# Layer 1's attention: two of four rows of probabilities transposed by VectorE and DMA instead of TensorE, with a fixed order of TensorE's work

## The chip, the cores and the metric

The kernel runs on one core of one Trainium2 chip. The core has five engines with queues of their own, each working through its instructions in order: TensorE (matrix products; PE in the profile, PEld for its weight loads), VectorE (DVE), ScalarE (ACT), GpSimd (POOL) and SyncE (SP, which only issues DMAs here). Engines wait for one another through semaphores. Tiles live in SBUF; TensorE writes to PSUM, of which this kernel makes eight banks of 128 x 512 float32. The metric is the device time of one execution in microseconds; lower is better. All data are float32.

## The reference, cut to what matters

Four layers over x of 4 x 512 x 256; each normalises x and adds an attention part and a feed-forward part that both read the same normalised x. Layer 1 has latent attention with 16 heads and, beside it, a gated feed-forward net together with a lookup of eight "experts" per token. The change is in its attention:

```python
# L1_attn: b = 4 sequences, s = 512 tokens, 16 heads, latent width 64, rope width 64
q = rmsnorm(x @ wq_a) @ wq_b              # 16 heads of 128 + 64
ckv = x @ wkv_a                           # latent 64 and rope keys 64, shared by all heads
kv = rmsnorm(ckv[..., :64]) @ wkv_b       # keys and values of each head
scores = einsum('bqhd,bkhd->bhqk', qf, kf) * 192 ** -0.5     # qf, kf: nope | rotated rope
probs = softmax(where(causal, scores, -inf))
out = einsum('bhqk,bkhd->bqhd', probs, v) @ wo

# L1_ffn: product-key lookup (8 of 512 experts per token) plus a gated net
x = x + L1_attn(xn) + L1_ffn(xn)
```

## The kernel before

**Streams.** Layer 1 is written as Python generators that issue instructions and yield an estimated cost. `weave` always advances the stream that is least far through its own total: the attention (`latent_pieces`, 457), the expert lookup (`product_key_pieces`, 237), the gated net (`glu_units`, 126) and, near the end, the first routing of layer 2 (`room`). A scheduler then orders the instructions of each engine by this order and by when it expects operands; an order may be forced with `tc.keep_in_program_order`, or with `c.chain`, which ties each instruction to the last chained one. In the kernel before, layer 3 alone uses `c.chain`.

**Attention.** The weights of keys and values are folded into the queries and the output, so all heads attend over the same latent keys `kf` and values `cv` (64 wide). The loop over s runs through 64 heads of one sequence each (4 groups of heads x 4 sequences x 2 pairs x 2). Two heads make a pair: `queries` (L1072 to L1085) projects for both, ScalarE copies the result to `pes`, four DMAs swap its halves into `psw`, and `rotate` (L1091 to L1094) applies the rotary embedding. Per head, four rows of blocks i = 0..3 ("rows one to four") have scores of 128, 256, 384 and 512 keys (L985). `exp_scores` takes the masked minimum on VectorE (L988) and the exponent with its sum on ScalarE (L992); a reciprocal (L1108) and ScalarE (L1110) scale the row to probabilities `pr0`..`pr3`.

**Transposes.** The product with the values needs the probabilities with keys on partitions. `turned` does this on TensorE for all ten 128 x 128 blocks (L1117), one column of blocks per PSUM bank `tr`, and copies each bank to `PT` (L1121) on VectorE (columns 0 and 2: 512 and 256 wide) or ScalarE (384 and 128 wide). After the second head of a pair, eight wide products give z of both heads, one head in each half of the bank (L1253):

```python
z[h * KL : (h + 1) * KL, j * P :], lhsT=cv[:, b * TPB + j, :],
rhs=PTs[s - 2 + h][:, START[j] : START[j] + SEQ - j * P],
```

ScalarE scales z into `zT` (L1259), and after every second pair the output product (L1267) is added to x on VectorE (L183).

**Beside it.** The expert lookup first routes on VectorE, then for 16 tiles of tokens gathers eight expert rows each by indirect DMA on GpSimd's queue into tiles `e` (L1371, eight buffers), takes eight dot products on VectorE (L1381) and adds eight scaled rows to x on VectorE (L177); each addition frees an `e` buffer for the next tile's gather. The gated net's products are L159 and L237.

**Layer 3** already transposes the probabilities by VectorE and DMA: VectorE turns 32 x 32 blocks into `Y` (L1598), four SyncE DMAs write `Y` to DRAM (L1603), and a fifth reads it back as `PT` (L1607); its value products are 128 wide (L1642).

Of the kernel before, what the change touches and what calls it, by code (L numbers as in the profile page):

```python
# [16 lines left out]
P = 128  # L17
NB, SEQ, DM = 4, 512, 256
# [12 lines left out]
class Ctx:  # L31


    def __init__(self, tc, stack):
        self.tc, self.nc = tc, tc.nc
        self.stack = stack
        self.n = 0
        pool = lambda name, **kw: stack.enter_context(tc.tile_pool(name=name, **kw))
        self.keep = pool("keep", bufs=1)
        self.ln = pool("ln", bufs=1)  # L40
        self.psum = pool("psum", bufs=4, space=bass.MemoryType.PSUM)
        self.users, self.then, self.later, self.pinned = {}, None, [], False
        self.trickle, self.chained = [], None

    def tile(self, pool, shape, tag, dtype=F32, **kw):
        self.n += 1
# [11 lines left out]
    def chain(self, ins):  # L58


        last, self.chained = self.chained, ins.ins
        if last is not None:
            self.tc.add_manual_dep(
                ins.ins, last.name,
                mybir.DependencyInfo(mybir.DependencyClass.NoSync, mybir.DependencyReason.DATA),
                reason="chain",
            )
        return ins
# [942 lines left out]

def latent_pieces(c, a, keep, open_pool):

# [45 lines left out]
    def queries(p):  # L1063

        g, b, pair = p // 8, p // 2 % 4, p % 2
        if p % 8 == 0:
            carry(g)
        wpe0, wpe1, wl0, wl1, _ = weights[g]
        tokens = slice(b * SEQ, (b + 1) * SEQ)
        cols = slice(pair * P, (pair + 1) * P)  # L1070
        pe, pl = c.ps(), c.ps()
        nc.tensor.matmul(pl, lhsT=wl0[:, cols], rhs=qa0[:, tokens], start=True, stop=False)  # L1072
        upper = nc.tensor.matmul(pe, lhsT=wpe1[:, cols], rhs=qa1[:KL, tokens], start=True, stop=False)
        with tc.issue_after(upper.ins), tc.high_priority(offset=200):
            nc.tensor.matmul(pl, lhsT=wl1[KL:, cols], rhs=qa1[KL:, tokens], start=False, stop=True)
        with tc.high_priority(offset=100):
            nc.tensor.matmul(pe, lhsT=wpe0[:, cols], rhs=qa0[:, tokens], start=False, stop=True)

        pes, psw = (c.tile(pool, [P, SEQ], n, bufs=1) for n in ("pes", "psw"))
        nc.scalar.copy(pes, pe)  # L1080
        for to in range(0, P, 32):
            nc.sync.dma_start(psw[to : to + 32, :], pes[to ^ 32 : (to ^ 32) + 32, :])
        qf = c.tile(pool, [P, 2, SEQ], "qf")
        nc.scalar.mul(qf[:KL, 0, :], pl[:KL, :], -scale)
        nc.scalar.mul(qf[KL:, 1, :], pl[KL:, :], -scale)  # L1085
        qfs[p] = qf
        return pes, psw, qf

    def rotate(pes, psw, qf):
        pec = c.tile(pool, [P, SEQ], "pec", bufs=1)  # L1090
        nc.vector.tensor_mul(pec, pes, cosq)  # L1091
        tc.keep_in_program_order(nc.vector.tensor_mul(psw, psw, sinq))
        nc.vector.tensor_add(qf[:KL, 1, :], pec[:KL, :], psw[:KL, :])
        nc.vector.tensor_add(qf[KL:, 0, :], pec[KL:, :], psw[KL:, :])  # L1094

    def probabilities(s, i):
        p, h = s // 2, s % 2
        b = p // 2 % 4
        if i == 0:
            totals[s] = c.tile(pool, [P, TPB], "total")  # L1100
        rinv = totals[s]
        prs[s].append(exp_scores(
            c, pool, late, qfs[p][:, h, :], kf[:, h, b * SEQ : (b + 1) * SEQ], i, rinv[:, i : i + 1]
        ))
        if i >= TPB - 2:

            done = slice(0, i + 1) if i < TPB - 1 else slice(i, i + 1)
            nc.vector.reciprocal(rinv[:, done], rinv[:, done])  # L1108
            for j in range(TPB)[done]:
                nc.scalar.mul(prs[s][j], prs[s][j], rinv[:, j : j + 1])  # L1110

    def turned(s, j):

        pt = c.ps("tr")
        n = SEQ - j * P
        for i in range(j, TPB):
            nc.tensor.transpose(  # L1117
                pt[:, (i - j) * P : (i - j + 1) * P], prs[s][i][:, j * P : (j + 1) * P], c.ident
            )
        copy = nc.scalar.copy if j % 2 else nc.vector.tensor_copy  # L1120
        return lambda: copy(PTs[s][:, START[j] : START[j] + n], pt[:, :n])  # L1121

    START = (0, 512, 896, 1152)
    qfs, prs, totals, PTs, zTs = {}, {}, {}, {}, {}
    rope = c.tile(pool, [P, SEQ], "psw", bufs=1)
    nc.scalar.dma_start(rope, a["l_rope"])
# [2 lines left out]
    def latents(b):  # L1129

        if b < 2:
            rooms = [c.tile(pool, [P, 1280], "PT")[:, :1024]]
        elif b == 2:
            rooms = [c.tile(pool, [P, SEQ], "zT", bufs=3) for _ in range(2)]
        else:
            rooms = [c.tile(pool, [P, 2, SEQ], "qf").rearrange("p a b -> p (a b)")]
        return [v3(r, QL + KL)[:, t, :] for r in rooms for t in range(TPB // len(rooms))]
# [35 lines left out]
    for b in range(NB):  # L1173
        tokens = slice(b * SEQ, (b + 1) * SEQ)
        lats.append(latents(b))
        for t in range(TPB):
            tt = b * TPB + t
            pl = c.ps()[:, : QL + KL]
            project_tokens(c, pl, wa, slice(0, QL + KL), slice(tt * P, (tt + 1) * P))
            lat = lats[b][t]  # L1180
            nc.vector.tensor_copy(lat, pl)
            sq = c.tile(pool, [P, QL + KL], "pr1")
            nc.scalar.activation(
                sq[:, :QL], lat[:, :QL], AF.Square, accum_out=ms[:, 0, tt : tt + 1]
            )
            nc.scalar.activation(
                sq[:, QL:], lat[:, QL:], AF.Square, accum_out=ms[:, 1, tt : tt + 1]
            )
            yield 0.85
            if t == 1 and b > 0:  # L1190
                yield from rotary_keys()

        pk = c.ps()
        project(c, pk, wa, slice(256, 384), tokens)
        rot = c.tile(pool, [P, SEQ], "pr3")
        nc.vector.tensor_mul(rot, pk, rope)
        rots.append((rot, tokens))
        yield 1.2
# [16 lines left out]
        finish(b)  # L1215
        yield 1.9

    copy = None
    yield 1.9
    for s in range(65):  # L1220
        if s < 64:
            prs[s] = []
        for i in range(TPB):
            if s < 64:
                probabilities(s, i)
            if s > 0:
                if i == 0:
                    PTs[s - 1] = c.tile(pool, [P, 1280], "PT")
                ready, copy = copy, turned(s - 1, i)
                if ready:  # L1230
                    ready()
            if i == 0 and s % 2 == 1 and s < 63:
                rotate(*turning)
            yield 0.85
            if i == 1 and s % 2 == 0 and s < 62:
                turning = queries(s // 2 + 1)
                yield 2.6
        if copy:
            copy()
            copy = None  # L1240
        if s > 0:
            del prs[s - 1]
        if s % 2 == 1:
            continue
        if s == 0:
            continue

        p = s // 2 - 1
        g, b, pair = p // 8, p // 2 % 4, p % 2
        z = c.ps("acc")  # L1250
        for j in range(TPB):
            for h in range(2):
                tc.keep_in_program_order(nc.tensor.matmul(  # L1253
                    z[h * KL : (h + 1) * KL, j * P :], lhsT=cv[:, b * TPB + j, :],
                    rhs=PTs[s - 2 + h][:, START[j] : START[j] + SEQ - j * P],
                    start=(j == 0), stop=(j == TPB - 1),
                ))
        zTs[pair] = c.tile(pool, [P, SEQ], "zT", bufs=3)
        nc.scalar.mul(zTs[pair], z, kv_w)  # L1259
        yield 2.1  # L1260
        if pair == 1:
            wz = weights[g][4]
            for t in range(0, TPB, 2):
                po = v3(c.ps("acc"), DM)
                for j in range(2):
                    for k in range(2):
                        nc.tensor.matmul(  # L1267
                            po[:, j, :], lhsT=zTs[k][:, (t + j) * P : (t + j + 1) * P],
                            rhs=wz[:, k, :], start=(k == 0), stop=(k == 1),
                        )  # L1270
                add_pair(c, b * TPB + t, po)
                if g == 3 and t == TPB - 2:
                    c.part_done(b)
                yield 1.7


def product_key_pieces(c, a, keep, pool, dram, xn):
# [131 lines left out]
def layer1(c, a, xn, following):  # L1409


    with ExitStack() as stack, ExitStack() as right:
# [4 lines left out]
        glu = pool_of("g1", 1)  # L1417
        dram = pool_of("p_dram", 1, space=bass.MemoryType.DRAM)
        keep = pool_of("l_keep", 1)
        latent = latent_pieces(c, a, keep, lambda: pool_of("l_h", 2))  # L1420

        def glu_units():
            same = dict(tanh=True, bufs=5)
# [989 lines left out]
```

## Time and profile before

| | |
|---|---|
| median of 10 runs | 2938.59 us (2935.44 to 2944.33) |
| the profiled execution | 2938.87 us, of which the span of its instructions is 2937.1 us |
| layer 1's heads in it | first scores 854 us, last value product 1476 us |
| 862 to 1029 us | before the expert gathers' dot products; VectorE busy 131.5 of 167 us |
| 1029 to 1404 us | dot products and gathers; VectorE busy 306.8 of 375 us |
| 1404 to 1476 us | last heads; VectorE busy 46.8 of 72 us |

Times in the profile are those of one execution, in us, single instructions in ns. A group's line reads: line of the kernel, engine, operation, output tile <- input tiles, shapes, count | busy us, mean ns of one | idle time of the engine before them, with what ended it. A float32 product is two instructions (two passes); a transpose is one. The chain of waits follows the work that ended last back through what released it. "us to landing" of a DMA counts from its issue to the arrival of its data.

### The profile page before, as it was taken

What the parts mean: (1) busy time and instruction counts of PE and PEld (TensorE: products, weight loads), DVE (VectorE), ACT (ScalarE), POOL (GpSimd) and SP (SyncE); (2) the same over time, 40 slices, a digit from 0 to 9 for tenths busy, and PEclk for the clock granted to TensorE, in tenths of its full rate; (3) what the DMA queues carried; (4) which work ended last, traced back from release to release, by engine and by line L of the source; (5) the groups of instructions that cost most, each with busy time, mean ns of one, the idle gap of its engine ahead of it and who ended that gap; (6) DMA issues with size and microseconds to landing.
All of it is one profiled execution on the core that took longest, in us unless ns stands there. A gap on an engine that the chain in (4) does not pass through costs nothing.

```text
span 2937.1 us, 40559 instructions
## 1 busy us (share of the span) xinstructions
PE 2883.5 (98%) x13812; PEld 1954.8 (67%) x13812; DVE 2134.5 (73%) x5434; ACT 1391.2 (47%) x3336; POOL 858.3 (29%) x681
## 2 busy tenths in 40 slices
PE   8999999999999999999999999999999999999999
PEld 5666665666755655555677688888888756666666
DVE  6877778787778787878765877777777666666666
ACT  4444445354376666667633554544454333333332
POOL 0565655656410033333035200000000043333331
PEclk9999999999999999999999999999999999999999
DMA  3333332332320134444235434444444200000000
GB/s 134 100 100 122 100 110 94 105 122 83 115 68 15 56 102 131 106 106 111 77 91 162 150 113 126 138 133 128 147 122 148 94 1 22 22 22 22 22 1 29
DMA packets 138366, 268.03 MB, mean 91 GB/s; under 512 B 19664, under 2 KB 99040, under 8 KB 133808
## 3 DMA queue, kind: packets, MB, share of 16 engines
q1 hardware_dynamic: 123696, 217.65, 23.7%
q0 software_dynamic: 14176, 47.01, 6.3%
q8 instruction: 109, 1.79, 0.2%
q14 instruction: 97, 0.79, 0.1%
q10 hardware_dynamic: 288, 0.79, 0.1%
HBM read 202.21 MB, written 54.26 MB: 87 GB/s over the span
## 4 chain that ended last, share of the span: by engine, by line
PE 84%; DVE 7%; ACT 3%; DMA 2%; POOL 1%; issue 1%; SPq 0%; ACTq 0%; DVEq 0%; POOLq 0%
PE mm L329 17%; PE mm L159 14%; PE mm L985 7%; PE acc L329 7%; PE tr L329 6%; PE acc L1642 5%; PE acc L1001 4%; PE tr L823 3%; PE acc L1253 2%; PE mm L167 2%; PE acc L237 2%; PE tr L237 2%; PE acc L801 2%; PE tr L1117 2%; PE acc L1267 1%; PE mm L2036 1%
## 5 line engine op out<-in xcount | busy, mean ns | idle before, releaser
L992 ACT ACTIVATE pr<-pr,nm 128x128 f32<-128x128 f32 (+3 forms) x512 | 286.1, 559 | 295.2 <-DVE nm L988 292.4
L988 DVE CUSTOM_DVE_ANT_0 pr<-mm,late 128x128 f32<-128x128 f32 (+3 forms) x512 | 245.4, 482 | 114.1 <-PE mm L985 112.4
L159 PE MATMUL mm<-xnT,wu 128*128 128x512 f32 x624 | 288.4, 600 | 0.0
L340 ACT COPY part<-mm 128x512 f32<-128x512 f32 (+1 forms) x372 | 177.8, 479 | 213.2 <-PE mm L329 205.1
L329 PE MATMUL mm<-token_sums,unit_sums 128*128 128x512 f32 (+1 forms) x624 | 267.5, 511 | 2.2 <-ACT part L340 2.2
L1371 POOL DMA_INDIRECT e<-in_p_experts,ids x128 | 130.6, 1021 | 464.6 <-DVE x L177 323.5
L159 PE MATMUL mm<-xnT,w_in 128*128 128x512 f32 x512 | 229.2, 593 | 0.6 <-DVE cy L591 0.6
L491 DVE SCALAR_TENSOR_TENSOR x<-acc,cw,x 128x128 f32<-128x128 f32 x372 | 128.7, 346 | 108.1 <-PE acc L329 106.5
L591 DVE SCALAR_TENSOR_TENSOR cy<-mm,ws,cy 128x509 f32<-128x509 f32 (+2 forms) x216 | 160.1, 744 | 51.5 <-ACT cy L587 47.5
L159 PEld LDWEIGHTS mm<-xnT,wu 128*128 128x128 f32 x624 | 115.8, 193 | 118.4 <-issue 110.4
L985 PE MATMUL mm<-kf,qf 128*128 128x128 f32 (+3 forms) x512 | 174.3, 443 | 3.4 <-DVE qf L1094 3.1
L761 POOL TENSOR_TENSOR G<-G,CB 128x1024 f32<-128x1024 f32 x64 | 151.5, 2367 | 82.1 <-DVE G L724 76.0
L744 ACT ACTIVATE xD<-xc,ws 128x128 f32<-128x128 f32 x256 | 83.9, 390 | 191.8 <-POOL y L785 182.4
L985 PE MATMUL mm<-k,q 128*128 128x128 f32 (+3 forms) x512 | 170.4, 437 | 3.7 <-DVE q L1542 3.4
L329 PEld LDWEIGHTS acc<-down_sums,hidden_sums 128*128 128x128 f32 x744 | 112.1, 192 | 85.1 <-issue 83.4
L159 PEld LDWEIGHTS mm<-xnT,w_in 128*128 128x128 f32 x512 | 96.5, 190 | 104.4 <-issue 94.9
L1642 PEld LDWEIGHTS acc<-PT,V 128*128 128x128 f32 x1280 | 154.5, 194 | 8.2 <-issue 4.9
L1642 PE MATMUL acc<-PT,V 128*128 128x128 f32 x1280 | 154.9, 277 | 3.5 <-DMA PT<-turned 3.5
L273 POOL TENSOR_TENSOR down_sums<-wu 128x256 f32<-128x256 f32 x8 | 5.9, 741 | 520.6 <-DMA wu<-in_o_units 520.6
L724 DVE TENSOR_TENSOR_SCAN G<-G,eye 128x1024 f32<-128x1024 f32 x64 | 148.1, 2315 | 0.0
L474 DVE TENSOR_TENSOR whole<-mm,part 128x512 f32<-128x512 f32 x128 | 88.5, 692 | 68.5 <-PE mm L329 68.1
L1117 PEld LDWEIGHTS tr<-con,pr 128*128 128x128 f32 x640 | 79.5, 142 | 83.0 <-issue 19.7
(440 smaller groups left out, 6770.8 us busy)
## 6 DMA issues: line engine op xcount, KB each, us to landing
turned<-Y SPq DMA_DIRECT2D x252, 160.0 KB, 2.6
PT<-turned SPq DMA_DIRECT2D x63, 640.0 KB, 3.9
G<-own SPq DMA_DIRECT2D x64, 512.0 KB, 4.5
w_in<-in_m_units SPq DMA_DIRECT2D x16, 1024.0 KB
eb<-since SPq DMA_DIRECT2D x96, 128.0 KB, 3.4
wu<-in_o_units SPq DMA_DIRECT2D x6, 1536.0 KB, 6.5
wo<-in_m_units SPq DMA_DIRECT2D x16, 512.0 KB, 13.0
psw<-pes SPq DMA_DIRECT2D x128, 64.0 KB, 3.2
```

What stands on the lines that cost most here:

```text
L159: c.nc.tensor.matmul(out, lhsT=w[:, d, cols], rhs=c.xnT[:, d, tokens], start=(d == 0), stop=(d == 1))
L329: self.kept(self.c.nc.tensor.matmul(bank, lhsT=lhsT, rhs=rhs, start=first, stop=True, skip_group_check=not first))
L340: self.c.nc.scalar.copy(r, bank)
L591: nc.vector.scalar_tensor_tensor(y[:, j:], src[:, : SEQ - j], conv[:, k, 3 - j : 4 - j], y[:, j:], ALU.mult, ALU.add,)
L724: tc.keep_in_program_order(nc.vector.tensor_tensor_scan(flat, flat, eye.rearrange("p h t -> p (h t)"), 0.0, ALU.mult, ALU.add))
L761: nc.gpsimd.tensor_mul(G, G, seqs[b][2][:, t, :][:, None, :].to_broadcast([P, HG, P]))
L985: kept(nc.tensor.matmul(sc, lhsT=q[:, i * P : n], rhs=k[:, :n], start=True, stop=True))
L988: nc.vector.tensor_tensor_reduce(out=pr, in0=sc, in1=late[:, SEQ - n :], scale=scale, scalar=-NEG, op0=ALU.add, op1=ALU.min, accum_out=nm,)
L992: nc.scalar.activation(pr, pr, AF.Exp, bias=nm, scale=-1.0, accum_out=total)
L1117: nc.tensor.transpose(pt[:, (i - j) * P : (i - j + 1) * P], prs[s][i][:, j * P : (j + 1) * P], c.ident)
L1371: nc.gpsimd.indirect_dma_start(out=e, out_offset=None, in_=a["p_experts"], in_offset=bass.IndirectOffsetOnAxis(ap=ids[:, t, k : k + 1], ax ...
L1642: kept(nc.tensor.matmul(zs[:, i], lhsT=head["V"][:, j, h, :], rhs=head["PT"][:, :, i * (i + 1) // 2 + j, :], start=(j == 0), stop=(j == i),))
```

## The change

- Rows three and four of each head's probabilities (seven of ten blocks) are no longer transposed by TensorE. `turn_strips` has VectorE turn 32 x 32 blocks into `Y`, SyncE write `Y` to DRAM in four DMAs, and GpSimd issue the DMA that reads it back into `PT`. The last head (s = 63) keeps TensorE for these rows.
- Rows one and two (three blocks) stay on TensorE, in one bank, copied by ScalarE. VectorE no longer copies from `tr`.
- All TensorE instructions of the attention are chained in program order, with `c.chain` now keeping one chain per engine; the four writes are chained on SyncE too. `queries` takes its two banks from `tr` instead of `mm`.
- The product with the values is now 20 products of 128 columns per pair, placed between the third and fourth scores of the odd head after next, and the output products follow in two pieces in the next even head.
- `pr0`..`pr3` have one buffer each, `PT` three, `Y` one, `zT` two; `rotate` works in place; the reciprocal is taken over two rows at a time.

```diff
-        last, self.chained = self.chained, ins.ins
+        last = self.chained.get(ins.ins.engine)
+        self.chained[ins.ins.engine] = ins.ins
...
-        pe, pl = c.ps(), c.ps()
...
+        pe, pl = c.ps("tr"), c.ps("tr")
+        for out, lhsT, rhs, start, stop in (
+            (pl, wl0[:, cols], qa0[:, tokens], True, False),
+            (pe, wpe1[:, cols], qa1[:KL, tokens], True, False),
+            (pl, wl1[KL:, cols], qa1[KL:, tokens], False, True),
+            (pe, wpe0[:, cols], qa0[:, tokens], False, True),
+        ):
+            c.chain(nc.tensor.matmul(out, lhsT=lhsT, rhs=rhs, start=start, stop=stop))
...
-        if i >= TPB - 2:
-            done = slice(0, i + 1) if i < TPB - 1 else slice(i, i + 1)
+            kept=c.chain, bufs=1,
+        if i % 2:
+            done = slice(i - 1, i + 1)
...
+    def wide(tile, i):
+        lo = 0 if i == 2 else 3
+        return tile[:, :896].rearrange("p (a j s) -> p j a s", j=7, s=32)[:, lo : lo + i + 1]
+    def turn_strips(s, i):
+        if i == 2:
+            Ys[s] = c.tile(pool, [P, 896], "Y", bufs=1)
+        nc.vector.transpose(wide(Ys[s], i), strips(prs[s][i]))
+        if i == TPB - 1:
+            room = c.tile(dram, [4, 32, 4, 224], "strips")
+            PTs[s] = c.tile(pool, [P, 1280], "PT", bufs=3)
+            Y = Ys.pop(s)
+            for a in range(4):
+                c.chain(nc.sync.dma_start(
+                    room[:, :, a, :].rearrange("b r e -> r b e"),
+                    Y[a * 32 : (a + 1) * 32].rearrange("p (b e) -> p b e", b=4),
+                ))
+            nc.gpsimd.dma_start(PTs[s][:, :896], room.rearrange("b r a e -> (b r) (a e)"))
+    def turned(s, rows):
...
+                c.chain(nc.tensor.transpose(
+                    pt[:, n * P : (n + 1) * P], prs[s][i][:, j * P : (j + 1) * P], c.ident
+                ))
...
+            return lambda: nc.scalar.copy(PTs[s][:, 896:], pt[:, : 3 * P])
...
+    def values(p):
+        z = c.ps("acc")
+        for i in range(TPB):
+            for j in range(i + 1):
+                for h in range(2):
+                    c.chain(nc.tensor.matmul(
+                        z[h * KL : (h + 1) * KL, i * P : (i + 1) * P], lhsT=cv[:, b * TPB + j, :],
+                        rhs=block(2 * p + h, i, j), start=(j == 0), stop=(j == i),
+                    ))
...
+    for s in range(66):
...
+            if i == 0:
+                if s % 2 == 1 and s < 63:
+                    rotate(*turning)
+                yield from islice(pieces, 1)
+            if i == 1 and s % 2 == 0:
+                yield from islice(pieces, 1)
+                if s < 62:
+                    turning = queries(s // 2 + 1)
+                    yield 2.6
+            if i == 2 and s % 2 == 1 and s > 2:
+                pieces = values(s // 2 - 1)
+                yield 2.6
+            if i == TPB - 1 and s < 63:
+                turn_strips(s, 2)
+                turn_strips(s, 3)
+            if s < 64 and i == TPB - 1:
+                copy = turned(s, (0, 1))
+            if s == 64 and i < 2:
+                copy = turned(63, (i + 2,))
```

## The prediction

> **What bounds the kernel now.** The page first: it gives the span of the one profiled execution, to which the sum is made (with 1.8 us outside it, 2938.87 us, 0.3 us above the median of 2938.59, so the two are used as one).
>
> ```profile
> span 2937.1 us, 40559 instructions
> PE 2883.5 (98%) x13812; PEld 1954.8 (67%) x13812; DVE 2134.5 (73%) x5434; ACT 1391.2 (47%) x3336; POOL 858.3 (29%) x681
> ```
>
> The change touches only layer 1's attention, whose 64 heads run from about 854 to 1476 us, so next the windows: before, during and after the stretch in which GpSimd gathers experts (columns: busy us and instructions of PE, PEld, DVE, ACT, POOL, then clock, DMA share, GB/s).
>
> ```profile
> 862.00:1029.00 167.00, 162.91 (x759) 98.10 (x758) 131.49 (x490) 110.22 (x300) 0.00 (x0) 0.99 0.12 33
> 1029.00:1404.00 375.00, 365.76 (x1620) 208.77 (x1619) 306.78 (x1040) 251.46 (x673) 123.05 (x121) 1.00 0.43 109
> 1404.00:1476.00 72.00, 70.37 (x348) 45.40 (x346) 46.78 (x166) 47.08 (x120) 0.55 (x1) 0.93 0.23 77
> ```
>
> TensorE looks 98% busy, but its ends are modelled. The chain of waits shows its real rate: four transposes 0.44 us, so 0.11 each; a 512-column pass 0.43. Adding up the columns streamed between 855 and 1476 us at these rates gives 538 of 621 us. So TensorE is the largest load (87%), VectorE the second (82% in the gather stretch), and the rest is latency. The chain of waits of the gather stretch says which:
>
> ```profile
> by line: PE mm L985 11.3%; PE acc L1253 8.7%; PE mm L159 8.6%; PE tr L1117 7.4%; DMA psw<-pes 6.9%; PE acc L1267 5.9%; PE acc L237 5.6%; ACT pr L992 4.6%; ACT pr L1110 4.0%; issue 3.6%; PE mm L1073 3.1%; DVE pr L988 3.1%; PE mm L1072 2.8%;
> ```
>
> A DMA holds 6.9% and the softmax steps on ScalarE and VectorE some 12%. By the timeline the widest scores of heads 1, 17 and 55 end at 862.8, 1028.0 and 1386.5 us: a pair of heads takes 20.6 us ahead of the gathers and 18.9 in them.
>
> **The change, part by part.**
>
> *TensorE.* Of ten transposes per head the seven of rows three and four go, in 63 heads: 441 x 0.11 = 48.5 us less. The product with the values becomes 20 narrow products per pair of heads in place of 8 wide ones. Columns are the same, instructions (two per float32 product) 40 in place of 16. The chain has both kinds, and the same half-width pairs in layer 0:
>
> ```profile
> 1307.45 0.44 PE tr L1117 x4
> 1318.37 2.30 PE acc L1253 x16
> 434.74 1.02 PE acc L801 x16
> ```
>
> 1.02/16 = 0.064 each makes 2.55 us per pair for 2.30 now: 32 x 0.25 = 8 us more. Net 40 us less TensorE work: 498 us, 15.6 per pair.
>
> *VectorE and ScalarE.*
>
> ```profile
> L988 DVE CUSTOM_DVE_ANT_0 pr<-mm,late 128x512 f32<-128x512 f32 x59 | 40.3, 682 | 2.3 <-PE mm L985 2.3
> L992 ACT ACTIVATE pr<-pr,nm 128x512 f32<-128x512 f32 x59 | 42.4, 719 | 9.8 <-DVE nm L988 8.6
> L1110 ACT ACTIVATE pr<-pr,total 128x384 f32<-128x384 f32 x59 | 35.4, 600 | 0.0
> L1110 ACT ACTIVATE pr<-pr,total 128x512 f32<-128x512 f32 x59 | 41.9, 709 | 3.0 <-DVE total L1108 3.0
> L1121 DVE COPY PT<-tr 128x512 f32<-128x512 f32 x59 | 40.5, 686 | 22.3 <-PE tr L1117 22.2
> L1121 DVE COPY PT<-tr 128x256 f32<-128x256 f32 x59 | 24.2, 411 | 5.6 <-PE tr L1117 5.6
> ```
>
> VectorE loses two copies per head (0.69 + 0.41 = 1.10 us) and gains two block transposes, which layer 3's timeline shows at 0.58 (384 columns) and 0.70 (512): +0.18 x 63 = 11 us more. ScalarE loses the 0.25 us copy of one block: 16 us less. At 68% it can take either. The rotation written in place and the two reciprocals of two columns each cost nothing either way.
>
> *The new round trip, which decides.* Rows three and four now leave through DRAM, and the products of a pair (in the fixed order: third step of the head after next) wait for them. So there is a loop: widest scores of the odd head, softmax, block transposes, four writes, one read, products of that pair, widest scores of the next odd head. Its stages:
>
> 1. Scores to last transpose. In the built order ScalarE does exponent of row four (0.72 + 0.19), exponent of the next head's row one (0.39 + 0.19), then the two scalings (0.60, 0.71); VectorE does the minimum before (0.68 + 0.08) and the last transpose after (0.70). That is 4.4 us with hand-overs; the dots and adds that stand between on VectorE add some 0.8. Taken 5.2.
> 2. Transpose to read: layer 3 does the same with SyncE.
>
> ```profile
> 1911.78 0.70 DVE L1598 STREAM_TRANSPOSE Y<-pr 128x512 f32<-128x512 f32 x1
> 1912.51 1.77 SPq L1603 DMA_DIRECT2D turned<-Y  x4
> 1916.56 0.34 SPq L1607 DMA_DIRECT2D PT<-turned  x1
> ```
>
> From 1912.48 to 1916.56 is 4.1 us, four issues and the last landing. On SyncE's queue the writes stand behind the rotation's four copies of the same head, done by then.
> 3. Read to landing. No such read from GpSimd is in the trace; the nearest rows are these.
>
> ```profile
> PT<-turned SPq DMA_DIRECT2D x63, 640.0 KB, 3.9
> e<-in_p_experts,ids POOLq DMA_INDIRECT x128, 4.5
> ```
>
> 448 KB by hardware queue would be at most 3.9 us, by GpSimd's queue 4.5 as a gather of 256 KB; taken 4.3 (nearer the row of the same queue).
>
> Sum 13.6 us. Then products 2.55, hand-over 0.1, widest scores 0.86 (two passes of 0.43), and other products that the built order puts between these two (31 pairs, mean 1.2 us, of which part lies ahead of the wait; taken 1.0): 18.1 us per pair. What TensorE has to do before the products (queries wait for the copy of rows one and two, about 4.2 us; queries 2.95; scores and transposes 3.1) takes 10.3 us and lies inside the 13.6, with room for most of the fillers. So the loop, not the 15.6 us of work, sets the pace.
>
> *The reads stand behind the gathers.* GpSimd works in order:
>
> ```profile
> 1228.69 0.95 POOL L1371 DMA_INDIRECT e<-in_p_experts,ids  x1 [12.80 <-DVE total L1108]
> 1229.94 0.95 POOL L1371 DMA_INDIRECT e<-in_p_experts,ids  x1 [0.30 <-DVE x L177]
> ```
>
> A gather every 1.25 us, eight in a burst. In the built order 13 of the 18 odd heads from 19 to 53 have their read behind two to eight gathers, set off by expert additions that start from 1.9 us before to 5.8 us after the last transpose on VectorE. Head 35: first addition at +0.9, eight gathers, 0.9 + 10.0 = 10.9, where the read could go at 4.1: 6.8 us late. So reckoned, heads 19, 21, 23, 25, 29, 31, 33, 35, 41, 43, 49, 51, 53 lose 1.5, 5.9, 6.5, 4.2, 4.1, 4.1, 6.5, 6.8, 6.4, 6.3, 0.2, 2.1, 6.2: 61 us. Even heads have nine more microseconds and lose nothing. While TensorE waits, VectorE catches up, so I take 50; the bounds are 0 (additions early) and 80 (the same plus 1.5 us per late read for data queued behind the gathers').
>
> [...]
>
> *The sum.* Ahead of the gathers, 8.5 pairs: 18.1 + 0.5 for expert routing on VectorE against 20.6: -17 us. In the gathers, 19 pairs: 18.1 + 0.4 for shared DMA against 18.9: -8, and +50. Heads 55 to 61, three pairs that took 62.5 us (by the timeline, widest scores at 1386.5 and 1449.0): 3 x (18.5 - 20.8) = -7. From head 61's scores to the end of the last products (1475.8) it takes 27 us now, and one more turn of the loop (18.1) with the last head's softmax, transposes, copies and products (4.4 + 0.8 + 1.1 + 2.6 = 8.9) makes 27 again. Total +18: 2957 us.
>
> **The rivals.**
>
> *A, the saving comes through (faster).* If additions run early and the reads land in 3.9, with 4.4 for the softmax, the loop is 12.4 + 3.5 + 0.6 = 16.5 and VectorE's 16.5 (306.8/19 + 0.35) with some waiting sets about 17.3: 8.5 x -3.3 = -28 ahead, 19 x -1.6 = -30 in the gathers, -10 after them, +40 for two thirds of the 61 us of late reads: 2911. For it: 40 us of TensorE work do go, and 6.9% of the chain was another DMA that stays off the path. Against it: every stage of the loop must run at its best. It decides once the loop stays under 17 us. This is the side that is not slower.
>
> *B, congestion.* Writes and reads add 2 x 448 KB per head, about 100 GB/s on the 109 of the gather stretch; writes, reads and the rotation's copies (3.7 us now) each take a microsecond longer, VectorE's order adds another: +2 per pair on 28 pairs, +56 on the forecast: near 3013. Against it: layer 3 (window of 1700 to 1900 us) moves 126 GB/s with landings of 2.6 and 3.9.
>
> *C, a wash.* The loop at 17.5 with the late reads as forecast (-0.6 x 31 = -19): 2938.
>
> *D, the change does not do what it says*: narrow products lose the pairing of halves and cost 40 x 0.108 = 4.3 us per pair, 56 us more. The 0.064 us of layer 0's row speaks against it; inside the chance of B.
>
> **How the numbers follow.** Forecast 0.48, B with D 0.15, A 0.29, C 0.08. 0.2% (6 us) is about what a measurement can tell from no change: faster 0.29, same 0.08, slower 0.63. The likeliest case alone runs from 2948 to 2990. The range reaches to just under A's time and into most of B: 2905 to 3010.
>
> **What would show it.** Right: "tr" transposes down to about 200; TensorE idle ahead of the products' first instruction, released by the DMA of the read, longest where a burst of gathers stands before it; pairs near 18 us ahead of the gathers and 20 to 22 in them; products at 0.064 us each; transposes at 0.58 and 0.70. Wrong: pairs near 17 us with VectorE or TensorE back to back (A); landings over 6 us (B); reads issued within 5 us of their transposes in most odd heads (the 50 us term falls).

## The result: slower, and by far more than forecast

The changed kernel takes 3083.86 us (median of 8 runs, 3077.99 to 3094.7) beside 2939.29 us of the kernel before in the same series: a ratio of 1.0492 (95% interval, given in brackets here and below, [1.048, 1.0503]), 145 us more. The forecast was +18 us, range 2905 to 3010. The direction was right and the size was not. The profiled execution has a span of 3080.6 us, 143.5 more than before; the readings below are from it. Each experiment further down is set against runs of the kernel before made beside it; that kernel took 2941 to 2945 us in some of these groups and 3010 to 3014 us in others, so only ratios are compared between groups, and between the two kinds to no better than 0.01 (the kernel with free order comes out at 1.0387 in one group and 1.0466 in another).

The head of the page, to be set against the two lines shown of before:

```profile
span 3080.6 us, 41983 instructions
```

The same windows as before, and a fourth for the heads that now run later (columns as there: PE, PEld, DVE, ACT, POOL, then clock, DMA share, GB/s):

```profile
862.00:1029.00 167.00, 147.20 (x765) 91.82 (x766) 126.68 (x468) 101.92 (x266) 8.10 (x15) 0.92 0.42 116
1029.00:1404.00 375.00, 274.27 (x1350) 170.16 (x1345) 238.38 (x766) 182.95 (x471) 106.16 (x119) 0.87 0.57 155
1404.00:1476.00 72.00, 61.54 (x321) 36.70 (x321) 56.49 (x182) 44.46 (x116) 28.28 (x30) 0.97 0.67 184
1476.00:1618.00 142.00, 114.28 (x620) 78.37 (x620) 83.46 (x281) 75.39 (x176) 14.97 (x21) 0.85 0.44 135
```

In the gather stretch no engine is full any more: TensorE 274 of 375 us (before 366), VectorE 238 (before 307), and the clock granted to TensorE is 0.87 where it was 1.00. The last value product ends at 1617.5 us instead of 1476.1. By the timeline, from widest scores to widest scores of odd heads, a pair takes 22.0 us in the eight pairs from head 1 (before 20.7), 24.6 in the nineteen from head 17 (18.9), 24.3 in the three from head 55 (20.8), and the tail from head 61 takes 37.0 (27.1): 11 + 110 + 10 + 10 = 141 of the 143.5 us.

The chain of waits of the gather stretch names two things that the same line of before did not lead with:

```profile
by line: DMA PT<-strips 16.0%; issue 15.8%; PE acc L1264 6.9%; PE mm L160 6.2%; PE acc L1281 5.5%; DVE x L178 5.2%; PE mm L986 4.8%; DMA strips<-Y 4.5%; DMA psw<-pes 3.3%; DVE pr L989 3.2%; POOL e L1421 3.0%; PE tr L1079 3.0%; ACT pr L993 2
```

The landing of the read is 16% of it. "issue" is time in which the profile shows no release; its longest piece, 16.4 us from 1134.9 us, ends in a gather on GpSimd's queue, ahead of a read; by GpSimd's timeline that gather had waited 16.6 us for an addition on VectorE. The waits of the heads (860 to 1618 us; total, times, longest):

```profile
POOL PT L1138 <- DMA strips<-Y: 151.1, 15, 25.1
PEld acc L1264 <- DMA PT<-strips: 115.7, 21, 13.6
PE acc L1264 <- DMA PT<-strips: 108.8, 19, 13.4
```

The first is GpSimd standing idle until a head's writes have landed. The last two are one wait seen by the weight load and by the product, so some 110 us of TensorE stand still ahead of and inside the products of a pair. In the kernel before no wait of the products for a DMA stands in this list. How a read comes to be late is seen on GpSimd's timeline:

```profile
1065.65 1.06 POOL L1421 DMA_INDIRECT e<-in_p_experts,ids  x1 [0.30 <-DVE x L178]
1067.01 0.95 POOL L1421 DMA_INDIRECT e<-in_p_experts,ids  x1 [0.30 <-DVE x L178]
...
1072.01 0.95 POOL L1421 DMA_INDIRECT e<-in_p_experts,ids  x1 [0.30 <-DMA strips<-Y]
1075.75 0.57 POOL L1138 DMA_DIRECT2D PT<-strips  x1 [2.79 <-issue]
```

Head 19's last block transpose ended at 1065.0; by stage 2 its read could go at 1069.1. It goes at 1075.75, behind six gathers and a wait of 2.79 us after them; in the chain of waits the head's own last write, issued at 1066.3, stands ahead of that read with 6.65 us, so slow writes are in this delay as well as the queue. The transfers of the gather stretch (median us from issue to landing, last column; the trace holds the landings of 21 of these reads, 13 of the writes, 8 of the copies to `psw` and 68 of the gathers):

```profile
PT<-strips POOLq DMA_DIRECT2D x31, 448.0 KB, 4.1
strips<-Y SPq DMA_DIRECT2D x120, 112.0 KB, 4.7
psw<-pes SPq DMA_DIRECT2D x57, 64.0 KB, 4.2
e<-in_p_experts,ids POOLq DMA_INDIRECT x88, 5.7
```

Over the whole kernel the writes land in 2.2 (median of 29 known landings); in this stretch it is 4.7, and a gather takes 5.7 where before's page has 4.5.

### The profile page after: what moved, and what is told of

It is laid out like the page before. It is cut to its first block, busy times and chain, and to the rows that moved or that the text cites. A ratio compares the mean times of both kernels' runs of the same rounds, so it can differ in the third digit from the quotient of the medians.

```text
span 3080.6 us, 41983 instructions
## 1 busy us (share of the span) xinstructions
PE 2881.2 (94%) x14139; PEld 1980.2 (64%) x14139; DVE 2154.6 (70%) x5432; ACT 1387.0 (45%) x3274; POOL 894.2 (29%) x744
## 4 chain that ended last, share of the span: by engine, by line
PE 76%; DVE 9%; DMA 5%; issue 3%; ACT 3%; POOL 2%; SPq 0%; DVEq 0%; ACTq 0%; POOLq 0%
PE mm L330 16%; PE mm L160 13%; PE mm L986 6%; PE acc L330 6%; PE tr L330 6%; PE acc L1693 5%; PE acc L1002 4%; PE tr L824 3%; DMA PT<-strips 3%; PE mm L168 2%; PE tr L238 2%; PE acc L802 2%; PE tr L1079 2%; PE acc L1264 1%; PE acc L1281 1%
## 5 line engine op out<-in xcount | busy, mean ns | idle before, releaser
L1264 PE MATMUL acc<-PT,cv 128*64 128x128 f32 x1280 | 106.2, 315 | 108.8 <-DMA PT<-strips 108.8
L986 PE MATMUL mm<-kf,qf 128*128 128x128 f32 (+3 forms) x512 | 183.0, 474 | 5.5 <-DVE qf L1095 4.8
L1264 PEld LDWEIGHTS acc<-PT,cv 128*64 128x64 f32 x1280 | 89.9, 159 | 134.2 <-DMA PT<-strips 115.7
L1138 POOL DMA_DIRECT2D PT<-strips x63 | 35.2, 559 | 410.4 <-DMA strips<-Y 151.1
```

Source lines behind the costliest of these rows:

```text
L986: kept(nc.tensor.matmul(sc, lhsT=q[:, i * P : n], rhs=k[:, :n], start=True, stop=True))
L1264: c.chain(nc.tensor.matmul(z[h * KL : (h + 1) * KL, i * P : (i + 1) * P], lhsT=cv[:, b * TPB + j, :], rhs=block(2 * p + h, i, j), start=(j ...
```

## The experiments

The theory after the profile: the round trip is in the loop and its reads come late. Rival 1: the fixed order itself costs. Rival 2: shared DMA, that is, transfers that slow one another.

**Reads on SyncE's queue.**

```diff
-            nc.gpsimd.dma_start(PTs[s][:, :896], room.rearrange(...))
+            c.chain(nc.sync.dma_start(PTs[s][:, :896], room.rearrange(...)))
```

> The 63 reads of turned rows move from GpSimd's queue to SyncE's, in the chain behind their own four writes; nothing else changes. Theory (the reads stand behind gathers in GpSimd's order): the read goes about 4.1 us after the last block transpose in nearly every odd head, where the kernel after has a mean of 8.6 in heads 19 to 53; about 4.5 x 18 = 80 us come back, 3000 us or a little less. Rival 1 (the fixed order itself costs, fillers do not fit): waits for the read shorten but pairs stay near 24 us, 3050 or more. Rival 2 (shared DMA): the read goes on time and lands in 6 us or more, 3030 to 3060.

Measured 3029.0 us, 1.0289 [1.0271, 1.0308]: 0.020 of the time before, about 60 us, come back. TensorE's order is nearly the same as in the kernel after, so this is close to the price of the queue alone. The wait of the products for the read over the heads (108.8 us in the kernel after), and the writes in the gather stretch:

```profile
PE acc L1264 <- DMA PT<-strips: 50.2, 16, 11.4
strips<-Y SPq DMA_DIRECT2D x136, 112.0 KB, 4.7
```

In odd heads 19 to 53 the read goes 6.3 us after the transposes (mean; 8.6 in the kernel after), not 4.1: with no gather ahead of it, its four writes still take 4.7 (median of 17 known landings). It lands little faster. The trace holds only two landings of these 18 reads (3.5 and 4.7 us), but the end of the products' wait tells when 13 of them had landed: after 6.0 us on average, against 6.7 for 15 of them in the kernel after. So the queue did delay the reads, as the theory says, but 80 us was too much, the slow transfers of rival 2 are there too, and more than half of the loss stays.

**Rows three and four back on TensorE, the chain kept.**

```diff
-            if i == TPB - 1 and s < 63:
-                turn_strips(s, 2)
-                turn_strips(s, 3)
-            if s == 64 and i < 2:
-                copy = turned(63, (i + 2,))
+            if 0 < s < 65 and i < 2:
+                copy = turned(s - 1, (i + 2,))
...
```

> Rows three and four are turned on TensorE again (no block transposes, no writes, no reads through DRAM; the copies of the turned rows split between ScalarE and VectorE); the fixed order and the 20 narrow products per pair stay. Theory (the way through DRAM and its reads are the cost, the order is not): 2940 to 2965 us, since the 48.5 us of transposes come back on TensorE and the narrow products cost about nothing. Rival 1 (fixed order): 3000 or more. Rival 2 (shared DMA): as the theory.

Measured 3070.58 us, 1.0435 [1.0417, 1.0452]. With no way through DRAM at all, nearly the whole loss is still there. The theory, as the only cause, falls; rival 1 (3000 or more) stands. The waits of this kernel's heads show what now holds TensorE: the scaling of the probabilities on ScalarE, ahead of the transposes.

```profile
PE tr L1147 <- ACT pr L1111: 97.4, 53, 4.2
```

**No gathers after the first tile of tokens.**

```diff
+        if t > 0:
+            rows[t, k] = rows[0, k]
+            return
         e = c.tile(pool, [P, 2 * DM], "e", bufs=8)
```

> The kernel after without the gathers of expert rows for all tiles of tokens but the first (their products read the rows of the first tile); this part of the computation is left out. Theory (reads behind gathers): the read goes 4.1 us after the last block transpose and lands in about 3.7, and about 80 to 100 us come back: 2980 to 3000. Rival 1 (fixed order): above 3040, since the order stays. Rival 2 (shared DMA): as the theory, and the reads' landing falls from 5.7 to under 4.

Measured 2981.34 us, 1.0132 [1.0114, 1.015]: 0.036 of the time before, about 105 us, come back, with chain and DRAM in place; rival 1 had forecast above 3040. The read goes 4.3 us after the transposes in odd heads 19 to 53, lands in 4.1 (all 18 known), and a pair takes 19.7. The transfers of 1029 to 1404 us:

```profile
strips<-Y SPq DMA_DIRECT2D x152, 112.0 KB, 2.1
PT<-strips POOLq DMA_DIRECT2D x38, 448.0 KB, 3.7
psw<-pes SPq DMA_DIRECT2D x76, 64.0 KB, 2.0
```

Writes and the rotation's copies took half the time without the gathers' traffic (2.1 and 2.0 us, where the kernel after has 4.7 and 4.2). So queue and traffic were both part of it. This edit also lets the order of everything else move, which is why it needs the control further down.

**Products one head later.**

```diff
-            if i == 2 and s % 2 == 1 and s > 2:
-                pieces = values(s // 2 - 1)
+            if i == 2 and s % 2 == 0 and s > 2:
+                pieces = values(s // 2 - 2)
...
```

> The products of a pair move one head later (third step of the even head two after), with a fourth buffer for the turned rows; for room the tokens' tile and the gate's tile have one buffer in place of two and the hidden tiles of a gated layer four in place of five. Reads stay on GpSimd's queue. Theory (the round trip is in the loop): the products wait no longer for the read, and 112 us of TensorE idle ahead of and inside the products go: 2930 to 2975. Rival 1 (fixed order): 3040 or more, idle moves to other waits. Rival 2 (shared DMA): as the theory, since a landing of 6 us is then hidden too.

Measured 3075.89 us, 1.0447 [1.043, 1.0465]. The theory misses. The wait for the read is gone from the list, and another stands in its place:

```profile
PE tr L1147 <- ACT pr L1111: 91.3, 29, 7.7
```

With the products out of the way the next instruction in the chain waits: the transposes, and the queries for a copy (23.7 us). Relieving one member of the chain only handed the wait to the next.

**TensorE's order free; rows on TensorE with free order; two buffers of probabilities.** These runs were made where the kernel before takes 3010 us; the two of the free order come again further down, where it takes 2941.

```diff
-                c.chain(nc.tensor.transpose(
+                free(nc.tensor.transpose(      # free = lambda ins: ins; so too scores, queries, products
```

```diff
-            kept=c.chain, bufs=1,
+            kept=c.chain, bufs=2,
```

> The kernel after, but layer 1's attention leaves TensorE's order free again (scores, transposes, queries, products and output products are no longer tied in one chain; the writes on SyncE's queue stay tied). The runs so far put the first theory in doubt: with rows three and four back on TensorE and no way through DRAM the kernel still took 3071 us. New theory (the chain of order on TensorE costs: a product or transpose that waits holds up all attention work behind it): 50 us or more come back, 3000 to 3030. Rival (single buffers of the probability rows hold the heads back, or the late reads do): no more than 20 us come back, 3060 or more.

> All rows turned on TensorE, as in the run before with that edit, and TensorE's order free. What is left of the change is then the single buffers, the placing of the steps and the narrow products. Theory of the chain: back to 2940 to 2970. Rival of the single buffers: 3030 or more.

> All rows turned on TensorE, the chain kept, but two buffers for each row of probabilities, as the kernel before has (for room the tokens' tile has one buffer, the gate's tile one, and the hidden tiles of a gated layer four in place of five). Theory of the chain: hardly changed, 3040 to 3070. Rival of the single buffers: 2940 to 2980.

> The kernel after with two buffers for each row of probabilities (the same room taken from the other tiles), chain and reads kept. Theory of the chain: 3050 to 3085. Rival of the single buffers: 2980 to 3020, the late reads remaining.

Measured 1.0387 [1.0367, 1.0406] for the free order, 1.0098 [1.0081, 1.0114] for rows on TensorE with free order, and for two buffers 1.0376 [1.0359, 1.0393] (rows on TensorE) and 1.0373 [1.0354, 1.0393] (rows by DMA). The single buffers are not the cause: with two of them most of the loss stays. The chain is, as long as the rows stay on TensorE (1.0376 to 1.0098); with the way through DRAM in place, the free order misses what its theory forecast, and the runs further down give the size.

**Both cures, and products later as well.**

> Both cures together: the reads on SyncE's queue (alone it took the ratio to the kernel before from 1.049 to 1.029) and TensorE's order free (alone 1.039). Theory (reads behind gathers on GpSimd's queue and the chain on TensorE each hold the heads up; with one gone the other sets the pace): ratio 1.00 to 1.012. Rival (the way through DRAM itself is too long for the loop): 1.02 or more.

> As the run before it, and the products of a pair one head later with a fourth buffer of turned rows (and the same smaller tiles as in the run that did this with the chain). Theory: the loop no longer holds the landing, and the 40 us of TensorE work saved show: ratio 0.985 to 1.0. Rival (later products only move the wait, single buffers or VectorE's order set the pace): 1.01 or more.

Measured 1.0323 [1.0303, 1.0342] and 1.0208 [1.0189, 1.0227]. Neither reaches the kernel before, and both miss their theory: with the chain gone and the reads on SyncE the kernel is still 3% slower. The rivals stand: for the first run, that the way through DRAM is too long for the loop. The runs without gathers below show where that is so.

**One part alone on the kernel before.** The chain on its scores, transposes, queries and products, in the order in which they are written (the queries lose their own priorities by it); and, separately, the narrow products.

```diff
-            nc.tensor.transpose(
+            c.chain(nc.tensor.transpose(       # so too scores, queries, products, output products
```

```diff
-                    z[..., j * P :], lhsT=cv[:, b * TPB + j, :], rhs=PTs[s - 2 + h][:, START[j] : START[j] + SEQ - j * P],
+                    z[..., i * P : (i + 1) * P], lhsT=cv[:, b * TPB + j, :], rhs=PTs[s - 2 + h][:, lo : lo + P],
```

> The kernel before with only one part of the change: its attention instructions on TensorE (scores, transposes, queries, products, output products) tied in one chain in the order in which they are written; everything else as before. Theory of the chain: 1.015 to 1.035. Rival (the chain costs only where the way through DRAM stalls it): 1.00 to 1.005.

> The kernel before with only the narrow products (20 of 128 columns per head in place of 4 of 512 to 128). By the profile after, a pair's 40 take 2.33 to 2.4 us when nothing stalls them, where the wide ones took 2.30: ratio 1.000 to 1.003. Rival (they fill TensorE's queue and cost the 0.25 us per pair forecast, or lose the halves' pairing): 1.003 to 1.02.

Measured 1.0374 [1.0356, 1.0392] for the chain alone and 1.0081 [1.0062, 1.01] for the narrow products alone. The chain alone loses most of what the whole change loses, more than its theory forecast. The narrow products cost more than expected (1.000 to 1.003).

**Side by side where the kernel before takes 2941 us.**

> The kernel after, unchanged, beside the next three so that the four can be compared directly. If the two costs overlap: 1.045 to 1.05, about 0.01 above either alone. If they add: 1.06 or more in company with the others' ratios of 1.037 to 1.039.

> The kernel after with TensorE's order free (way through DRAM alone, with the narrow products). Overlap: 1.035 to 1.04. If the chain is the whole cost: under 1.015.

> Rows on TensorE and free order: neither the chain nor the way through DRAM; the narrow products, single buffers and the placing of the steps remain. Overlap: 1.005 to 1.012. Rival (what remains costs most): 1.02 or more.

> The kernel before with the chain of order alone. Overlap: 1.03 to 1.04. If the chain costs little by itself: under 1.01.

| | order free | order chained |
|---|---|---|
| rows three and four on TensorE | 1.0072 [1.0055, 1.0088], 2961 us | 1.0435 [1.0417, 1.0452] (the run above), 3071 us |
| rows by VectorE and DMA | 1.0466 [1.0445, 1.0487], 3078 us | 1.0488 [1.0465, 1.051], 3085 us |

The kernel before with the chain alone: 1.0406 [1.0388, 1.0424], 3059 us. Free order with rows by DMA, and the chain alone, came out above the ranges expected for overlap (1.035 to 1.04 and 1.03 to 1.04). The two costs overlap. From the free kernel on TensorE the way through DRAM alone adds 117 us, the chain alone about 107 (0.0363 x 2941), both together 124. Either is enough; undoing one gives back 6 to 16 us. Three windows of the gather stretch, each its own kernel, say the same; first rows on TensorE with free order, then rows by DMA with free order, then the kernel before with the chain:

```profile
1029.00:1404.00 375.00, 361.23 (x2010) 222.50 (x2008) 283.08 (x944) 250.59 (x642) 118.37 (x120) 1.00 0.43 108
```

```profile
1029.00:1404.00 375.00, 296.34 (x1362) 177.45 (x1361) 236.59 (x768) 183.63 (x470) 109.54 (x121) 0.88 0.59 154
```

```profile
1029.00:1404.00 375.00, 328.77 (x1347) 180.66 (x1348) 258.89 (x865) 211.24 (x560) 94.52 (x96) 0.95 0.37 91
```

With rows by DMA and a free order the products still wait long for the reads (116.1 us in the kernel after beside it):

```profile
PE acc L1265 <- DMA PT<-strips: 93.8, 20, 11.1
```

The time of a pair of heads, counted as above in one execution of each kernel (in its other one the kernel after had 22.0 and 24.6), tells where each cost falls:

| us per pair | ahead of the gathers (heads 1 to 17) | in the gathers (17 to 55) |
|---|---|---|
| kernel before | 20.7 | 18.9 |
| rows on TensorE, order free | 19.9 | 20.0 |
| rows on TensorE, order chained | 23.1 | 23.4 |
| rows by DMA, order free | 19.5 | 24.8 |
| rows by DMA, order chained (this group) | 21.4 | 25.0 |
| kernel before with the chain | 23.3 | 22.8 |

Ahead of the gathers the way through DRAM costs nothing, and the chain is the cost. In the gathers each costs 3 us or more by itself, and with the way through DRAM in place the chain adds next to nothing.

What the chain does is seen in one row, of the kernel before and then of the same kernel chained (heads only):

```profile
PEld tr L1117 <- ACT pr L1110: 16.1, 52, 0.9
```

```profile
PEld tr L1119 <- ACT pr L1112: 81.7, 118, 3.0
```

With a free order TensorE has other attention work ahead of the transposes while ScalarE scales; in the chain all of it stands behind them. Only the order in which the program is written was tried as a chain; whether another fixed order would cost as much, no run shows.

**The gathers, with a control.** The same gathers left out of the kernel before, and of the kernel after with free order.

> The kernel before without the gathers of expert rows for all tiles of tokens but the first (that part of the computation is left out). The gathers are off its path: 0.99 to 1.00.

> The kernel after with TensorE's order free and without the same gathers. Theory (gathers delay the reads on GpSimd's queue and every transfer by their traffic, the way through DRAM is else short enough): pairs near 19.5 us throughout, 0.99 to 1.005. Rival (the way through DRAM is too long with or without them): 1.02 or more.

Measured 0.9906 [0.9883, 0.993] and 1.0016 [0.9998, 1.0034]. Against its control the change without chain and gathers costs 1.0016 / 0.9906 = 1.011, with chain 1.0132 / 0.9906 = 1.023 (from two groups of runs), in company with the gathers 1.047 and 1.049. Without the gathers a pair of the free kernel takes 19.2 us between heads 17 and 55, as the expectation had it (19.5), and one of the control 18.4. So the gathers turn a cost of 1 to 2% into one of 5%.

## Why the prediction was wrong

By its own steps:

- *TensorE's transposes* (441 fewer): right. 199 are left in the heads. *Block transposes* at 0.58 and 0.70: right, 0.574 and 0.686.

```profile
L1128 DVE STREAM_TRANSPOSE Y<-pr 128x512 f32<-128x512 f32 x63 | 43.2, 686 | 0.3
L1147 PE MATMUL tr<-con,pr 128*128 128x128 f32 x199 | 36.3, 287 | 11.5 <-ACT pr L1111 10.5 <-ACT xnT L152 0.6 <-ACT pes L1082 0.2
```

- *Narrow products* at 2.55 per pair: too high for the instructions (2.33 when nothing stalls them, in the chain of waits of the kernel with rows on TensorE). Alone they cost 0.8% all the same, about 24 us where 8 were forecast. The order of the other instructions moves with them, and I take that to be the price; no run separates it.
- *"What TensorE has to do before the products ... lies inside the 13.6, with room for most of the fillers"*: this step failed. It priced the fixed order at nothing. The chain alone costs 118 us on the kernel before (3059 less 2941). Ahead of the gathers the read went 4.4 us after the transposes and landed in 3.9 (forecast 4.1 and 4.3), and the round trip was 15.3 us (five heads whose landing is known; the step from scores to transposes took 7.2, not 5.2); a pair took 22.0, not 18.6. With the order free, and the rows still by DMA, it took 19.5. So there the order is most of the miss, some 20 of 28 us (11 more in place of 17 less).
- *"The reads stand behind the gathers"*, 61 us taken as 50: the right mechanism, and about the right size for the queue alone. In the 18 odd heads the reads went 82 us later in all than 4.1 after the transposes, 16 of 18 after more than 5 us; but with the reads on SyncE, where no gather stands ahead of them, they still went 39 us late. So about half of the 82 is the queue, and the rest goes with slow writes, as far as the trace tells, which stage 2 had at layer 3's speed. "While TensorE waits, VectorE catches up" was wrong: VectorE was held as well, and its busy time in that stretch fell from 307 to 238 us. By experiment the queue cost about 60 us of the kernel's time.
- *Landing 4.3 + 0.4*: mis-sized. It was 5.7 in the seven of those heads whose landing the trace holds, 6.7 in 15 of them by the end of the products' wait, and the writes took 4.7 (2.6 in layer 3). Rival B's mechanism was there, at more than its "a microsecond longer", and so was its sign, landings over 6 us. This term and the one before carry the miss in the gathers, the largest part of all (110 us more where 42 were forecast): scores to transposes 5.3 (as forecast), read 8.6 later, landing 6.7 make 20.6 of the 24.6 us of a pair, and the 4.0 left are about the 4.5 that the forecast had for the products and what follows. The loop did set the pace there; its stages were longer. The row that had stood nearest, a gather's 4.5, was the kernel before's, and was 5.7 in the gather stretch of the kernel after, where 155 GB/s moved and not 109.
- *Heads 55 to 61, -7, and tail, 0*: +10 and +10. The last gather goes at 1499.9, ahead of these heads. One read among them, issued at 1521.5 right behind a load of weights on GpSimd's queue, took 11.7 us to land, and the products waited for it; this is about the first +10. The second was not taken apart.
- *The rates of TensorE* were taken as fixed at the full clock. They were not (last section): about 46 us of TensorE's time (57.7 less 11.7), of which no run tells how much lies on the path.

The terms cannot simply be added: in the table each of the two large costs alone makes nearly the whole loss. By the pairs, in the gathers, where most of the loss is, the loop through DRAM sets the pace with the chain or without it (25.0 and 24.8). What stays open is how much of the 117 us of the way through DRAM with free order is the order that the scheduler then chooses; every edit but the one of the queue moves much of that order. With the gathers gone, chain and way through DRAM together cost about 2%, so the round trip as forecast (13.6; 14.3 measured there in odd heads 19 to 53) was nearly right for a kernel without that load.

No version tried that does all of the work beats the kernel before.

## What to carry to other kernels

A fixed order on one in-order engine can have a price of its own (118 us here), even when every instruction in it is cheap: cost it as a change by itself, by asking of each member what it waits for and what then stands behind it. A transfer that a loop waits for should not stand on a queue with long bursts of others (60 us here), and its stages are to be priced at the traffic that the change creates, not at the one before (the writes took 4.7 us here, layer 3's 2.6). Where two delays lie on the same loop, removing one can show little (6 to 16 us here): test them in a two-by-two, and read it stage by stage.

## What the runs showed of the hardware

**A stall cost TensorE twice.** At 1172.3 us of the kernel after TensorE stands still for 2.5 us, waiting for a read; then eight 512-column passes of the gated net take 5.19 us, where they take 3.44 at 1087.1 us, at a clock of 1.00. Windows of 1 us of the kernel after (the first figure behind the length is PE busy, the third from the end is the clock):

```profile
1174.00:1175.00 1.00, 0.25 (x2) 0.19 (x2) 0.00 (x0) 0.00 (x0) 0.00 (x0) 0.98 0.31 106
1175.00:1176.00 1.00, 1.00 (x3) 0.50 (x2) 0.99 (x2) 0.00 (x0) 0.55 (x1) 0.50 0.04 8
1178.00:1179.00 1.00, 1.00 (x3) 0.45 (x2) 0.00 (x0) 0.22 (x1) 0.00 (x0) 0.81 0.84 280
1179.00:1180.00 1.00, 1.00 (x4) 0.38 (x2) 0.59 (x1) 0.38 (x1) 0.00 (x0) 1.00 1.09 314
```

The clock is 0.50 from 1175 to about 1178.4. From 860 to 1620 us the kernel after has 25 such spells, the kernel before 6, the one with the chain alone 21, the one with rows on TensorE and free order 2; they last 3.4 us or a multiple of it. Adding up (1 - clock) x PE busy over slices of 1 us, TensorE loses 57.7 us by them, before 11.7, with the chain alone 43.8, rows on TensorE and free order 5.0. With rows on TensorE and a free order it was busy for 361 of the 375 us of the gather stretch, at a clock of 1.00; with rows by DMA and a free order, where the products wait for reads, there were 18 spells and 47.0 us.

The spells begin and end on a grid of 3.41 us in the clock's record of the kernel after and of the one before, and the clock in them is 0.50. What went with a spell was the idle time within one step of the grid, not always one long stall: in the kernel with the chain alone, with its 21 spells, a single stall of TensorE was over 3 us (3.68, by its modelled ends). In the kernel after, each of the 25 spells follows a step in which TensorE, by its modelled ends, was idle for 1.7 us or more, half of the step, and no step after which the clock stayed full had over 1.8 us. With the chain alone, 19 of the 21 follow a step with 1.4 us or more, and the full clock stayed after at most 1.7; the other two follow steps with no idle time by the modelled ends. In the kernel before two of the six follow steps with 1.2 and 2.4 us, and the full clock stayed after at most 1.5; the other four follow steps with 0.6 us or less, made up mostly of products of 8 or 23 columns (21 to 30 of them in a step). That the modelled ends of such short products overlap and hide idle time is an assumption of mine; no run shows it.

**GpSimd's DMA instructions took about as long as before**: a gather's 0.95 us (median) and 1.46 at most in the kernel after, 0.95 and 1.45 before, and a read's 0.56 and 0.61.
